# A graph-attention block with a quantised feed-forward on one core: the opening loads, the fill of the head pairs, the second layer norm and the last product rearranged

## The chip, the core and the metric

The kernel runs on one core of one Trainium2 chip. A core has five engines that run their own instruction streams and wait for one another by semaphores: TensorE (PE in the profile; its weight loads are PEld), VectorE (DVE), ScalarE (ACT), GpSimd (POOL) and SyncE (SP, which here only issues DMAs). The metric is the device time of one execution in microseconds (us). Three executions before the change took 384.24, 382.71 and 383.2 us; their median is 383.2 us.

## The reference

Inputs are x (384 x 1024), 6528 edges (`src`, `dst`, `edge_type_5`), and weights; all is f32.

```python
x = x + gnn(layernorm(x));  x = x + ffn(layernorm(x))

# gnn: q, k, v = x @ w.T + b, then a second projection each, 16 heads of 64
q2 = (q @ wiq.T + biq); k2 = (k @ wik.T + bik); v2 = (v @ wiv.T + biv)
mask = full((384, 384), -inf);  mask[src, dst] = softplus(edge_type_weights)[edge_type - 1]
# an empty diagonal place gets softplus(edge_type_weights)[3]; of equal edges the last one counts
attn = softmax(q2 @ k2.T / 8 + mask);  out = (attn @ v2) @ wo.T + bo

# ffn: fake quantisation of the activations by ONE scale over the whole tensor, weights row by row
def act_quant(x, clip): s = sigmoid(clip) * max(abs(x)) / 127; return clip(round(x / s), -128, 127) * s
h  = act_quant(silu(xq @ wg.T) * (xq @ wu.T), clip_down)       # xq = act_quant(x, clip_x), 352 wide
out = h @ wd.T
```

The scale over the whole tensor is a barrier: no element can be quantised before the largest of all is known.

## The kernel before

Rows are handled in three tiles of 128 (`NT`), features in eight blocks of 128 (`KC`). It runs in these stages.

**Opening (0 to 24 us).** SP issues the loads of x tile 0, x tile 1, `wq` blocks 0 and 1, x tile 2, and the other `wq` blocks (L83 to L87 and `load_w`), each 128 x 1024 f32 (512 KB). POOL issues seven small loads (L100 to L105): the rows of the biases, four edge-type weights and two clip factors, each of these three spread to all partitions by the DMA, and three lists of edges. While x arrives PE does 36 transposes of an identity (`WARM`). For each tile `row_stats` (L277) takes mean and reciprocal deviation on DVE (bn_stats, bn_aggr, `rstd_of`, whose square root is on ACT), and `normalise` (L284) writes the normalised rows on DVE (L288), turns them on PE four blocks at a time (L295) and copies each four from PSUM on ACT (L296). `q_first` (L300) multiplies the turned tile with `wq` blocks 0 and 1. The argument `between` puts the statistics of the next tile between the two groups of four; for tile 1 it is `edges_and_stats` (L317): edges to float, the key `384 * src + dst`, its way over memory back to all partitions (POOL, L323 and L257), and the statistics of tile 2.

**Projections (24 to 163 us).** `project2` (L178) computes two output blocks with seven products of half size in place of eight (Winograd's form of Strassen); `left_sums` and `right_sums` are its sums on DVE. Meanwhile DVE and POOL build the mask in memory (`tables`, `mask_groups`).

**Head pairs (163 to 333 us).** Eight pairs `p` of heads. PE's order is written out by hand: scores of pair p (L603) with softmax on DVE (L609, L623) and ACT (L613); transposes and weighted sums of pair p-1 (`weigh`, L633, L635, L641, L645); and between them `fill`, cut in sixteenths by `fill_to` (L694): for even p the product for v2 (L580), for odd p up to 5 the seven products of `inner_k` for the k2 of the next two pairs (L189, 29 steps), for p = 7 part of the output projection (L651). `prepare` puts the quantisation of the feed-forward weights in between (L496 to L542). The order on DVE and ACT in this stage follows from the program's order by a planner. The first product of `project2` goes from PSUM to SBUF on ACT (L203), and its PSUM buffer, one of two named mm, is the one that the third product writes.

**Output projection and second layer norm (333 to 357 us).** Per tile, PE finishes the output projection group by group (L801), and `residual` (L745) on DVE adds x and takes the row maximum (L747), bn_stats in pieces of 256 columns (L752) and the row minimum (L753); `normalise` (L755) ends with two DVE instructions per tile that write the normalised row (L787). Tile 2 has groups of 512, 256 and 256 columns in two PSUM buffers (mm). `turn` transposes each tile, `keep_busy` (L844) issues transposes whose result nobody reads, and `all_max` (L127) takes the largest value over all partitions.

**Feed-forward (357 to 384 us).** Gate and up products (L882), the second scale, and the product with wd (L929): six groups of 128 x 512, each scaled on DVE (L933), added to x on POOL (L938, first three) or DVE (L943, last three) into a tile `o` with three buffers, and stored by SP.

Of the kernel before, what the change touches and what calls it, by code (L numbers as in the profile page):

```python
# [23 lines left out]
F32 = mybir.dt.float32  # L24
# [37 lines left out]
def gnn_ffn_kernel(ctx: ExitStack, tc: tile.TileContext, a: dict, out: bass.AP):  # L62
# [18 lines left out]


    x = act.tile([P, NT, F], F32, name="actT")  # L83
    for t in range(NT):
        if t == NT - 1:
            wq_first = [load_w("wq", o) for o in range(FIRST)]
        nc.sync.dma_start(x[:, t, :], a["x"][t * P : (t + 1) * P, :])  # L87
    bias_rows = const.tile([5 * KC, P], F32)
    etw = const.tile([P, 4], F32)
    clip = const.tile([P, 2], F32)  # L90
    biv_b = const.tile([P, F], F32)


# [46 lines left out]

    ident_b = const.tile([P, P], BF16)
    later = ph1.tile([P, GROUP * P], F32, name="later", bufs=1)
    bias = const.tile([P, 5 * KC], F32)
    w8 = const.tile([P, 4], F32)

    def right_sums(src, pool, name, in_place=True):
# [90 lines left out]
    def run(steps):  # L237
        for _ in steps:
            pass
# [6 lines left out]
    with ph1_stack:  # L246
# [37 lines left out]
        def normalise(t, between=None):  # L284
            xn = rows_p.tile([P, F], F32, name="row")
            for j in range(2):
                hs = slice(j * 512, (j + 1) * 512)
                nc.vector.tensor_scalar(  # L288
                    xn[:, hs], x[:, t, hs], mv1[:, t, 0:1], rstd1[:, t : t + 1], op0=ALU.subtract, op1=ALU.mult
                )  # L290
            for g in range(2):
                pt = ps_tp.tile([P, 4, P], F32, name="tp")
                for j in range(4):
                    c = 4 * g + j
                    nc.tensor.transpose(pt[:, j, :], xn[:, c * P : (c + 1) * P], ident)  # L295
                nc.scalar.copy(xnT[:, 4 * g : 4 * g + 4, t * P : (t + 1) * P], pt)  # L296
                if g == 0 and between:
                    between()

# [10 lines left out]
        for _ in range(WARM):  # L310
            nc.tensor.transpose(pt, ident, ident)
        row_stats(0)
        normalise(0, lambda: row_stats(1))
        q_first(0, 0)
        q_first(1, 0)

        def edges_and_stats():  # L317

            nc.vector.tensor_copy(edges_f, edges_i)
# [8 lines left out]
        normalise(1, edges_and_stats)  # L328
        q_first(0, 1)
        q_first(1, 1)  # L330
        normalise(2)

        wneg = small.tile([P, 4], F32, name="wneg")
        nc.vector.tensor_scalar(wneg, etw, -1.0, None, op0=ALU.mult)
# [6 lines left out]
        pt = ps_tp.tile([P, 512], F32, name="tp")  # L341
        nc.tensor.transpose(pt[:, : 5 * KC], bias_rows, ident[: 5 * KC, : 5 * KC])
        wq_next = [load_w("wq", o) for o in (2, 3)]
        sums_next, steps = left_sums(*wq_next, ph1)
        run(steps)
        nc.vector.tensor_copy(bias, pt[:, : 5 * KC])
        x_right, steps = right_sums(xnT, ph1, "x_right", in_place=False)
        run(steps)
        q_first(0, 2)
# [194 lines left out]
    with ExitStack() as ph:  # L544
# [122 lines left out]
        for p in range(NP):  # L667
# [77 lines left out]
        def residual(t, col, c0, width, pm, st, hi, lo):  # L745
            cs = slice(c0, c0 + width)
            nc.vector.tensor_tensor_reduce(  # L747
                x[:, t, cs], pm[:, :width], x[:, t, cs], 1.0, -3.0e38, op0=ALU.add, op1=ALU.max,
                accum_out=hi[:, col : col + 1],
            )  # L750
            for c in range(c0, c0 + width, 256):
                nc.vector.bn_stats(st[:, c // 256, :], x[:, t, c : c + 256])  # L752
            nc.vector.tensor_reduce(lo[:, col : col + 1], x[:, t, cs], axis=AX.X, op=ALU.min)  # L753

        def normalise(t, last, st, hi, lo):  # L755

            mv = small.tile([P, 2], F32, name="mv2")
            nc.vector.bn_aggr(mv, st.rearrange("p a b -> p (a b)"))
            mean = mv[:, 0:1]
            var = small.tile([P, 1], F32, name="var2")  # L760
            nc.vector.tensor_scalar(var, mv[:, 1:2], EPS, None, op0=ALU.add)
            s0 = small.tile([P, 1], F32, name="s2")
# [12 lines left out]
            nw = small.tile([P, 1], F32, name="nw2")  # L775
            nc.vector.tensor_scalar(nw, vr, -0.5, 1.5, op0=ALU.mult, op1=ALU.add)
            rstd = small.tile([P, 1], F32, name="rstd2")
            nc.vector.tensor_mul(rstd, nw, r0)
            if t == 0:
                nc.vector.tensor_mul(row_max[:, 0:1], far, rstd)  # L780
            else:
                nc.vector.tensor_scalar(
                    row_max[:, t : t + 1], far, rstd, row_max[:, t - 1 : t], op0=ALU.mult, op1=ALU.max
                )
            for g in range(2):
                gs = slice(g * 512, (g + 1) * 512)
                nc.vector.tensor_scalar(xn[:, t, gs], x[:, t, gs], mean, rstd, op0=ALU.subtract, op1=ALU.mult)  # L787


        for t in range(NT):  # L790
            groups = [(0, 512), (512, 512)] if t < NT - 1 else [(0, 512), (512, 256), (768, 256)]
            st = small.tile([P, 4, 6], F32, name="st2")
            hi = small.tile([P, 3], F32, name="hi")
            lo = small.tile([P, 3], F32, name="lo")
            for g, (c0, width) in enumerate(groups):
                pm = open_groups.get((t, g)) if t < NT - 1 else None
                ks = [NP - 1]
                if pm is None:
                    pm, ks = ps_mm.tile([P, 512], F32, name="mm"), range(KC)
                for k in ks:  # L800
                    nc.tensor.matmul(  # L801
                        pm[:, :width], outT[:, k, t * P : (t + 1) * P], wo[k][:, c0 : c0 + width],
                        start=(k == 0), stop=(k == KC - 1),
                    )
                residual(t, g, c0, width, pm, st, hi, lo)
                if g == 1 and len(groups) == 3:
                    nc.vector.tensor_tensor(hi[:, 0:1], hi[:, 0:1], hi[:, 1:2], op=ALU.max)
                    nc.vector.tensor_tensor(lo[:, 0:1], lo[:, 0:1], lo[:, 1:2], op=ALU.min)
            normalise(t, len(groups) - 1, st, hi, lo)
        run(prep)  # L810

# [1 line left out]
    with ExitStack() as ph:  # L813
# [109 lines left out]
        for t in range(NT):  # L923
            ts = slice(t * P, (t + 1) * P)
            for g in range(2):
                gs = slice(g * 512, (g + 1) * 512)
                pm = ps_mm.tile([P, 512], F32, name="mm")
                for ic, (i0, rows) in enumerate(ICS):
                    nc.tensor.matmul(  # L929
                        pm, hq[:rows, ic, ts], wdT[:rows, ic, gs], start=(ic == 0), stop=(ic == 2)  # L930
                    )
                y = ff.tile([P, 512], F32, name="y", bufs=6)
                nc.vector.scalar_tensor_tensor(y, pm, sh, wd_scale_b[:, gs], op0=ALU.mult, op1=ALU.mult)  # L933
                if len(last) or t * 2 + g == 3:
                    last.append((t, gs, y))
                else:
                    o = ff.tile([P, 512], F32, name="o")
                    nc.gpsimd.tensor_add(o, x[:, t, gs], y)  # L938
                    nc.sync.dma_start(out[t * P : (t + 1) * P, gs], o)

        for t, gs, y in last:
            o = ff.tile([P, 512], F32, name="o")
            nc.vector.tensor_add(o, x[:, t, gs], y)  # L943
            nc.sync.dma_start(out[t * P : (t + 1) * P, gs], o)


# [45 lines left out]
```

## Time and profile before

| what | value |
|---|---|
| median of three executions | 383.2 us (382.71 to 384.24) |
| the profiled execution | 385.56 us, of which the span is 383.8 us |
| PE busy, share of the span | 364.5 us, 95% |
| DVE, ACT, POOL busy | 261.1, 107.2, 74.6 us |
| granted TensorE clock, mean | 0.986 of full speed |
| read from memory | 41.91 MB |

Times in the profile count from the start of the span. "Busy" of PE is modelled from pipelined matmuls, so that a wait inside a group shows as a longer group. A line like `[3.67 <-ACT k L203]` gives the time that an engine stood idle before an instruction and what released it. The chain of waits is followed back from the last instruction; 70% of it is PE, 14% DVE, 7% DMA and 5% ACT.

### The profile page before, as it was taken

Reading aid. Unit: us, or ns where it says so; the run is one execution under the profiler, and the core shown is the slowest. Engines: PE = TensorE matmul, PEld = TensorE weight load, DVE = VectorE, ACT = ScalarE, POOL = GpSimd, SP = SyncE. Lnnn points to the kernel's source line nnn. Section 1 sums busy time; section 2 is a strip of 40 time slices with the busy share of each in tenths; the row PEclk is TensorE's granted clock in tenths of the full one; section 3 lists DMA queues with packets and bytes.
Section 4 is the critical chain, followed back from the end, with each engine's and each line's share of the span. In section 5 each row is a group of like instructions: output and inputs, shape, how many; then the busy total and the mean of one; then the engine's idle time right before and its main releaser. Section 6 shows DMA issues by size and latency. Waiting matters only on the chain.

```text
span 383.8 us, 5838 instructions
## 1 busy us (share of the span) xinstructions
PE 364.5 (95%) x2101; PEld 301.2 (78%) x2101; DVE 261.1 (68%) x785; ACT 107.2 (28%) x256; POOL 74.6 (19%) x81
## 2 busy tenths in 40 slices
PE   7999999999999999989879999999999999998973
PEld 7899999999999998987676859686776545457661
DVE  5878888888879987976657366726583430298784
ACT  2252100000000010144553545536443524001330
POOL 6100354455545543400000000000000000000003
PEclk9999999999999999999989999999999999999996
DMA  8996333343343456283440030140394000000004
GB/s 239 375 397 212 114 111 110 113 130 111 110 123 110 145 174 206 57 273 106 146 129 3 19 130 19 38 147 0 118 371 130 6 0 2 0 0 1 2 1 164
DMA packets 17804, 44.50 MB, mean 116 GB/s; under 512 B 3262, under 2 KB 8400, under 8 KB 17392
## 3 DMA queue, kind: packets, MB, share of 16 engines
q1 hardware_dynamic: 15104, 39.46, 30.5%
q0 software_dynamic: 2672, 4.68, 4.1%
q8 instruction: 16, 0.26, 0.3%
q14 instruction: 12, 0.10, 0.1%
HBM read 41.91 MB, written 2.21 MB: 115 GB/s over the span
## 4 chain that ended last, share of the span: by engine, by line
PE 70%; DVE 14%; DMA 7%; ACT 5%; issue 2%; POOL 0%; SPq 0%; DVEq 0%; ACTq 0%
PE p L189 33%; PE mm L580 7%; PE mm L189 6%; PE tp L633 4%; PE mm L651 3%; PE sc L651 3%; PE mm L303 3%; PE sc L641 3%; PE sc L603 3%; DMA row<-in_L_ffn_w_down_dram 2%; DMA wt<-in_wik_dram 2%; ACT e L613 2%; DVE e L623 2%; DVE s L609 1%; DMA row<-in_L_ffn_w_gate_dram 1%
## 5 line engine op out<-in xcount | busy, mean ns | idle before, releaser
L425 POOL DMA_INDIRECT mask_d<-value,place x51 | 59.3, 1162 | 62.1 <-DVE place L422 47.0
L189 PE MATMUL p<-actT,wt 128*128 128x192 f32 x360 | 65.8, 326 | 0.0
L189 PEld LDWEIGHTS p<-actT,wt 128*128 128x128 f32 x360 | 59.7, 190 | 0.0
L580 PE MATMUL mm<-wt,actT 128*128 128x256 f32 x192 | 46.1, 384 | 0.0
L580 PEld LDWEIGHTS mm<-wt,actT 128*128 128x128 f32 x192 | 34.8, 190 | 7.8 <-issue 2.2
L613 ACT ACTIVATE e<-s,mn 128x384 f32<-128x384 f32 x48 | 29.0, 605 | 31.1 <-DVE mn L609 29.5
L609 DVE CUSTOM_DVE_ANT_0 s<-sc,mask 128x384 f32<-128x384 f32 x48 | 24.6, 550 | 13.1 <-PE sc L603 13.0
L818 POOL MEMSET hT<- 128x384 f32 x1 | 0.4, 418 | 163.7 <-PE sc L641 163.7
L189 PE MATMUL p<-x_right,s 128*128 128x192 f32 x176 | 32.2, 326 | 0.0
L189 PE MATMUL p<-x_right,wt 128*128 128x192 f32 x176 | 32.2, 326 | 0.0
L189 PEld LDWEIGHTS p<-x_right,s 128*128 128x128 f32 x176 | 29.2, 190 | 0.0
L189 PEld LDWEIGHTS p<-x_right,wt 128*128 128x128 f32 x176 | 29.2, 190 | 0.0
L635 ACT COPY eTs<-tp 128x384 f32<-128x384 f32 x48 | 20.7, 481 | 28.0 <-PE tp L633 27.9
L412 DVE SCALAR_TENSOR_TENSOR junk<-key_b,key,later 128x384 f32<-128x384 f32 (+3 forms) x51 | 27.5, 540 | 0.0
L200 DVE SCALAR_TENSOR_TENSOR actT<-p,bias,actT 128x192 f32<-128x192 f32 x45 | 18.7, 416 | 8.5 <-PE p L189 4.8
L189 PE MATMUL mm<-actT,wt 128*128 128x192 f32 x96 | 20.7, 344 | 4.0 <-ACT k L203 4.0
L203 ACT COPY actT<-p 128x192 f32<-128x192 f32 x15 | 4.8, 320 | 66.1 <-PE p L189 66.1
L189 PEld LDWEIGHTS mm<-actT,wt 128*128 128x128 f32 x96 | 15.9, 196 | 8.3 <-ACT k L203 4.9
L603 PE MATMUL sc<-k,actT 64*128 64x384 f32 x96 | 21.7, 521 | 0.1
L633 PEld LDWEIGHTS tp<-ident,e 128*128 128x128 f32 x144 | 17.2, 141 | 5.0 <-issue 2.6
L213 ACT ACTIVATE actT<-p,bias 128x192 f32<-128x192 f32 x15 | 6.3, 421 | 52.7 <-PE p L189 34.8
L633 PE MATMUL tp<-ident,e 128*128 128x128 f32 x144 | 20.0, 275 | 0.3 <-ACT eTs L635 0.3
(210 smaller groups left out, 589.7 us busy)
## 6 DMA issues: line engine op xcount, KB each, us to landing
wt<-in_wq_dram SPq DMA_DIRECT2D x8, 512.0 KB
wt<-in_wk_dram SPq DMA_DIRECT2D x8, 512.0 KB
wt<-in_wv_dram SPq DMA_DIRECT2D x8, 512.0 KB
wt<-in_wiq_dram SPq DMA_DIRECT2D x8, 512.0 KB
wt<-in_wik_dram SPq DMA_DIRECT2D x8, 512.0 KB
wt<-in_wiv_dram SPq DMA_DIRECT2D x8, 512.0 KB
wt<-in_wo_dram SPq DMA_DIRECT2D x8, 512.0 KB
actT<-in_x_dram SPq DMA_DIRECT2D x6, 512.0 KB
```

The costliest lines, as they stand in the source:

```text
L189: nc.tensor.matmul(z, left[:, k * P : (k + 1) * P], r[:, k, :], start=(k == 0), stop=(k == HK - 1))
L200: nc.vector.scalar_tensor_tensor(dst, z, b, with_, op0=ALU.add, op1=ALU.add)
L303: nc.tensor.matmul(pm_first[o][:, ts], wq_first[o][:, k * P : (k + 1) * P], xnT[:, k, ts], start=(k == 0), stop=(k == KC - 1),)
L412: nc.vector.scalar_tensor_tensor(junk[:, :left], keys[:, (c - k0) * P : (c - k0) * P + left], key[:, c : c + 1], later[:, :left], op0=ALU. ...
L425: ins = nc.gpsimd.indirect_dma_start(out=mask_d, out_offset=bass.IndirectOffsetOnAxis(ap=place[:, c : c + 1], axis=0), in_=value[:, c : c ...
L580: nc.tensor.matmul(pm, vT[:, k, t * P : (t + 1) * P], wt[k // HK][:, k0 : k0 + 256], start=(k == 0), stop=(k == KC - 1),)
L603: nc.tensor.matmul(ps[t, h], q2[hs, t * P : (t + 1) * P], k2[hs, :], start=True, stop=True)
L609: nc.vector.tensor_tensor_reduce(s, ps[t, h], mask[:, t, :], -SCALE, 3.0e38, op0=ALU.add, op1=ALU.min, accum_out=mn[h][:, t : t + 1],)
L613: nc.scalar.activation(e[h][:, t, :], s, AF.Exp, bias=mn[h][:, t : t + 1], scale=-1.0, accum_out=sm[h][:, t : t + 1],)
L633: nc.tensor.transpose(pt[:, t * P : (t + 1) * P], e[h][:, t, m * P : (m + 1) * P], ident)
L635: nc.scalar.copy(eT[h][m], pt)
L651: nc.tensor.matmul(pm, outT[:, k, t * P : (t + 1) * P], wo[k][:, gs], start=(k == 0), stop=(k == KC - 1))
```

## The change

- *Opening.* x tile 0 is loaded as two halves of 64 partitions, the lower by SP and the upper by ACT. POOL's seven small loads move behind the statistics of tile 1: a POOL copy of tile 1's mean and variance (`loaded`) comes first, then the edges, the biases, the weights and the clip factors. The last two go into one row of six numbers on one partition, and a matmul with a row of ones spreads them over the partitions, into the PSUM tile that holds the turned biases; one DVE copy takes both. Tile 0's copies from PSUM (L296) are cut in two. The edge work moves behind the statistics of tile 2.
- *Head pairs.* `fill_to(2)` becomes `fill_to(3)` for odd p.
- *Second layer norm.* bn_stats takes 512 columns at once for tiles 0 and 1. Their normalised rows are written by ACT in two passes (subtract, then scale), after one small DVE instruction for the negated mean. Tile 2 is cut into 512, 256, 128 and 128 columns, the last two in other PSUM buffers (sc), with bn_stats of 128 columns. The first `keep_busy` has 14 transposes and not 18.
- *Last product.* The groups alternate between PSUM buffers mm and x, and the sums are written over `y`, without the tile `o`.

```diff
+    half = P // 2
+    nc.scalar.dma_start(x[half:, 0, :], a["x"][half:P, :])
     for t in range(NT):
         if t == NT - 1:
             wq_first = [load_w("wq", o) for o in range(FIRST)]
-        nc.sync.dma_start(x[:, t, :], a["x"][t * P : (t + 1) * P, :])
+        rows = half if t == 0 else P
+        nc.sync.dma_start(x[:rows, t, :], a["x"][t * P : t * P + rows, :])
...
-    nc.gpsimd.dma_start(bias_rows, a["biases"])
-    nc.gpsimd.dma_start(etw, row_bcast(a["L0_gnn_edge_type_weights"], 4))
-    nc.gpsimd.dma_start(clip[:, 0:1], row_bcast(a["L0_ffn_clip_x"], 1))
-    nc.gpsimd.dma_start(clip[:, 1:2], row_bcast(a["L0_ffn_clip_down"], 1))
-    for j, name in enumerate(("src", "dst", "edge_type_5")):
-        nc.gpsimd.dma_start(edges_i[:, j, :], a[name].rearrange("(c p) -> c p", p=P))
+    nc.gpsimd.memset(ones, 1.0)
...
-                nc.scalar.copy(xnT[:, 4 * g : 4 * g + 4, t * P : (t + 1) * P], pt)
+                step = 2 if t == 0 else 4
+                for j in range(0, 4, step):
+                    c = 4 * g + j
+                    nc.scalar.copy(xnT[:, c : c + step, t * P : (t + 1) * P], pt[:, j : j + step, :])
...
-        normalise(0, lambda: row_stats(1))
+        def stats_and_loads():
+            row_stats(1)
+            loads = [(edges_i[:, j, :], a[n].rearrange("(c p) -> c p", p=P)) for j, n in enumerate(("src", "dst", "edge_type_5"))]
+            loads.append((bias_rows, a["biases"]))
+            for c0, n, name in ((0, 4, "L0_gnn_edge_type_weights"), (4, 1, "L0_ffn_clip_x"), (5, 1, "L0_ffn_clip_down")):
+                loads.append((row[:, c0 : c0 + n], a[name].rearrange("(a n) -> a n", a=1)))
+            nc.gpsimd.tensor_copy(loaded, mv1[:, 1, :])
+            for dst, src in loads:
+                nc.gpsimd.dma_start(dst, src)
+        normalise(0, stats_and_loads)
...
-        def edges_and_stats():
+        def stats_and_edges():
+            row_stats(2)
             nc.vector.tensor_copy(edges_f, edges_i)
...
-            row_stats(2)
...
         normalise(2)
+        pt = ps_tp.tile([P, 512], F32, name="tp")
+        nc.tensor.transpose(pt[:, :NB], bias_rows, ident[:NB, :NB])
+        nc.tensor.matmul(pt[:, NB : NB + 6], ones, row, start=True, stop=True)
...
+        nc.vector.tensor_copy(bias, pt[:, : NB + 6])
...
-            fill_to(2)
+            fill_to(3 if p % 2 else 2)
             prepare(2)
             next(sc)
...
-            for c in range(c0, c0 + width, 256):
-                nc.vector.bn_stats(st[:, c // 256, :], x[:, t, c : c + 256])
+            for c in range(c0, c0 + width, part):
+                nc.vector.bn_stats(st[:, c // part, :], x[:, t, c : c + part])
...
+            if t < NT - 1:
+                minus = small.tile([P, 1], F32, name="minus")
+                nc.vector.tensor_scalar(minus, mean, -1.0, None, op0=ALU.mult)
             for g in range(2):
                 gs = slice(g * 512, (g + 1) * 512)
-                nc.vector.tensor_scalar(xn[:, t, gs], x[:, t, gs], mean, rstd, op0=ALU.subtract, op1=ALU.mult)
+                if t < NT - 1:
+                    nc.scalar.activation(xn[:, t, gs], x[:, t, gs], AF.Identity, bias=minus)
+                    nc.scalar.activation(xn[:, t, gs], xn[:, t, gs], AF.Copy, scale=rstd)
+                else:
+                    nc.vector.tensor_scalar(xn[:, t, gs], x[:, t, gs], mean, rstd, op0=ALU.subtract, op1=ALU.mult)
...
-            groups = [(0, 512), (512, 512)] if t < NT - 1 else [(0, 512), (512, 256), (768, 256)]
+            if t < NT - 1:
+                groups, part = [(0, 512), (512, 512)], 512
+            else:
+                groups, part = [(0, 512), (512, 256), (768, 128), (896, 128)], 128
...
-                    pm, ks = ps_mm.tile([P, 512], F32, name="mm"), range(KC)
+                    pool, name = (ps_mm, "mm") if g < 2 else (ps_sc, "sc")
+                    pm, ks = pool.tile([P, 512], F32, name=name), range(KC)
...
-        keep_busy(18, ps_x, "x")
+        keep_busy(14, ps_x, "x")
...
-                pm = ps_mm.tile([P, 512], F32, name="mm")
+                pool, name = (ps_mm, "mm") if g == 0 else (ps_x, "x")
+                pm = pool.tile([P, 512], F32, name=name)
...
-                    o = ff.tile([P, 512], F32, name="o")
-                    nc.gpsimd.tensor_add(o, x[:, t, gs], y)
-                    nc.sync.dma_start(out[t * P : (t + 1) * P, gs], o)
+                    nc.gpsimd.tensor_add(y, x[:, t, gs], y)
+                    nc.sync.dma_start(out[t * P : (t + 1) * P, gs], y)
...
-            o = ff.tile([P, 512], F32, name="o")
-            nc.vector.tensor_add(o, x[:, t, gs], y)
-            nc.sync.dma_start(out[t * P : (t + 1) * P, gs], o)
+            nc.vector.tensor_add(y, x[:, t, gs], y)
+            nc.sync.dma_start(out[t * P : (t + 1) * P, gs], y)
```

In the planner's order after the change, ACT's copy L203 of an odd pair stands behind the first two exponentials of that place and ahead of the other four; before, six (p = 1) or five (p = 3, 5) exponentials stand ahead of it.

More of the change, by code (lines that the diff above doesn't have):

```diff
@@ L86, in gnn_ffn_kernel @@
             wq_first = [load_w("wq", o) for o in range(FIRST)]
-        nc.sync.dma_start(x[:, t, :], a["x"][t * P : (t + 1) * P, :])
+        rows = half if t == 0 else P
+        nc.sync.dma_start(x[:rows, t, :], a["x"][t * P : t * P + rows, :])
     bias_rows = const.tile([5 * KC, P], F32)
-    etw = const.tile([P, 4], F32)
-    clip = const.tile([P, 2], F32)
+    row = const.tile([1, 6], F32)
+    ones = const.tile([1, P], F32)
     biv_b = const.tile([P, F], F32)
@@ L142, in gnn_ffn_kernel @@
     later = ph1.tile([P, GROUP * P], F32, name="later", bufs=1)
-    bias = const.tile([P, 5 * KC], F32)
+    NB = 5 * KC
+    bias = const.tile([P, NB + 6], F32)
+    etw, clip = bias[:, NB : NB + 4], bias[:, NB + 4 : NB + 6]
     w8 = const.tile([P, 4], F32)
@@ L312, in gnn_ffn_kernel @@
         row_stats(0)
-        normalise(0, lambda: row_stats(1))
+        def stats_and_loads():
[7 more added lines that the diff above has]
+                nc.gpsimd.dma_start(dst, src)
+        loaded = small.tile([P, 2], F32, name="loaded")
+        normalise(0, stats_and_loads)
         q_first(0, 0)
         q_first(1, 0)
-        def edges_and_stats():
+        def stats_and_edges():
+            row_stats(2)
             nc.vector.tensor_copy(edges_f, edges_i)
@@ L325, in edges_and_stats @@
                 load_keys()
-            row_stats(2)
-        normalise(1, edges_and_stats)
+        normalise(1, stats_and_edges)
         q_first(0, 1)
@@ L331, in gnn_ffn_kernel @@
         normalise(2)
+        pt = ps_tp.tile([P, 512], F32, name="tp")
+        nc.tensor.transpose(pt[:, :NB], bias_rows, ident[:NB, :NB])
+        nc.tensor.matmul(pt[:, NB : NB + 6], ones, row, start=True, stop=True)
+        wq_next = [load_w("wq", o) for o in (2, 3)]
+        sums_next, steps = left_sums(*wq_next, ph1)
+        run(steps)
+        nc.vector.tensor_copy(bias, pt[:, : NB + 6])
         wneg = small.tile([P, 4], F32, name="wneg")
@@ L340, in gnn_ffn_kernel @@
         nc.scalar.activation(wln, wexp, AF.Ln, bias=1.0)
[L341 to L346, printed above, removed]
         x_right, steps = right_sums(xnT, ph1, "x_right", in_place=False)
@@ L743, in gnn_ffn_kernel, with residual @@
         open_groups = {(t, g): pm for t, g, pm in early}
-        def residual(t, col, c0, width, pm, st, hi, lo):
+        def residual(t, col, c0, width, part, pm, st, hi, lo):
             cs = slice(c0, c0 + width)
@@ L784, in normalise @@
                 )
+            if t < NT - 1:
+                minus = small.tile([P, 1], F32, name="minus")
+                nc.vector.tensor_scalar(minus, mean, -1.0, None, op0=ALU.mult)
             for g in range(2):
                 gs = slice(g * 512, (g + 1) * 512)
-                nc.vector.tensor_scalar(xn[:, t, gs], x[:, t, gs], mean, rstd, op0=ALU.subtract, op1=ALU.mult)
-        for t in range(NT):
-            groups = [(0, 512), (512, 512)] if t < NT - 1 else [(0, 512), (512, 256), (768, 256)]
-            st = small.tile([P, 4, 6], F32, name="st2")
-            hi = small.tile([P, 3], F32, name="hi")
-            lo = small.tile([P, 3], F32, name="lo")
+                if t < NT - 1:
[3 more added lines that the diff above has]
+                    nc.vector.tensor_scalar(xn[:, t, gs], x[:, t, gs], mean, rstd, op0=ALU.subtract, op1=ALU.mult)
+        for t in range(NT):
+            if t < NT - 1:
+                groups, part = [(0, 512), (512, 512)], 512
+            else:
+                groups, part = [(0, 512), (512, 256), (768, 128), (896, 128)], 128
+            st = small.tile([P, F // part, 6], F32, name=f"st2_{part}")
+            hi = small.tile([P, 4], F32, name="hi")
+            lo = small.tile([P, 4], F32, name="lo")
             for g, (c0, width) in enumerate(groups):
@@ L804, in gnn_ffn_kernel @@
                     )
[L805 to L808, printed above, removed]
+                residual(t, g, c0, width, part, pm, st, hi, lo)
+                if 0 < g < len(groups) - 1:
+                    nc.vector.tensor_tensor(hi[:, 0:1], hi[:, 0:1], hi[:, g : g + 1], op=ALU.max)
+                    nc.vector.tensor_tensor(lo[:, 0:1], lo[:, 0:1], lo[:, g : g + 1], op=ALU.min)
             normalise(t, len(groups) - 1, st, hi, lo)
@@ L933, in gnn_ffn_kernel @@
                 nc.vector.scalar_tensor_tensor(y, pm, sh, wd_scale_b[:, gs], op0=ALU.mult, op1=ALU.mult)
-                if len(last) or t * 2 + g == 3:
+                if t * 2 + g >= 3:
                     last.append((t, gs, y))
                 else:
-                    o = ff.tile([P, 512], F32, name="o")
-                    nc.gpsimd.tensor_add(o, x[:, t, gs], y)
-                    nc.sync.dma_start(out[t * P : (t + 1) * P, gs], o)
+                    nc.gpsimd.tensor_add(y, x[:, t, gs], y)
+                    nc.sync.dma_start(out[t * P : (t + 1) * P, gs], y)
         for t, gs, y in last:
-            o = ff.tile([P, 512], F32, name="o")
-            nc.vector.tensor_add(o, x[:, t, gs], y)
-            nc.sync.dma_start(out[t * P : (t + 1) * P, gs], o)
+            nc.vector.tensor_add(y, x[:, t, gs], y)
+            nc.sync.dma_start(out[t * P : (t + 1) * P, gs], y)
 def _out_blocks(w):
```

## The prediction

> **What bounds the kernel now.** I read the page first, for the shares; then the waits and the chain of waits, for the places where TensorE (PE) stands still; then the timeline and the windows around these places.
>
> ```profile
> span 383.8 us, 5838 instructions
> PE 364.5 (95%) x2101; PEld 301.2 (78%) x2101; DVE 261.1 (68%) x785; ACT 107.2 (28%) x256; POOL 74.6 (19%) x81
> PE 70%; DVE 14%; DMA 7%; ACT 5%; issue 2%; POOL 0%; SPq 0%; DVEq 0%; ACTq 0%
> ```
>
> PE is busy for 95% of the span: an edit is worth the PE idleness, or half-speed PE time, that it removes. Four stretches show that and are touched: the opening, the first product of the odd head pairs, the second layer norm with the scale behind it, and the last product. The timeline at pair 1 (start, us, engine, line, operation, and in brackets the idle time before it with its releaser):
>
> ```profile
> 189.46 1.46 PE L189 MATMUL mm<-k_right,s 128*128 128x192 f32 x8
> 194.59 0.92 PE L189 MATMUL mm<-actT,wt 128*128 128x192 f32 x4 [3.67 <-ACT k L203]
> 197.46 2.33 PE L189 MATMUL mm<-actT,s 128*128 128x192 f32 x8
> 199.62 0.60 PE L633 MATMUL tp<-ident,e 128*128 128x128 f32 x4
> 193.64 0.60 ACT L613 ACTIVATE e<-s,mn 128x384 f32<-128x384 f32 x1
> 194.24 0.29 ACT L203 COPY k<-mm 128x192 f32<-128x192 f32 x1
> ```
>
> PE idles 3.67 us until ACT's copy L203 frees a PSUM buffer; that copy, 0.29 us long, is queued behind exponentials whose scores come late from DVE. The windows beside it (PE, PEld, DVE, ACT, POOL busy; granted clock; DMA share; GB/s):
>
> ```profile
> 191.00:194.60 3.60, 0.01 (x1) 0.01 (x1) 2.99 (x11) 2.84 (x10) 0.00 (x0) 1.00 0.11 44
> 195.80:199.20 3.40, 3.40 (x14) 3.40 (x13) 1.44 (x3) 0.96 (x2) 0.00 (x0) 0.50 0.69 217
> 374.00:375.00 1.00, 1.00 (x4) 0.30 (x2) 0.13 (x2) 0.00 (x0) 1.00 (x2) 0.50 0.00 0
> ```
>
> The stall is followed by 3.4 us of PE work at a granted clock of 0.50; the last product runs at 0.50 too. Then, on PE and DVE, the stalls of later pairs, the second layer norm and the last product, and links of the chain of waits:
>
> ```profile
> 227.48 2.59 PE L603 MATMUL sc<-k,actT 64*128 64x384 f32 x8
> 262.62 1.94 PE L603 MATMUL sc<-k,actT 64*128 64x384 f32 x8
> 348.21 3.72 PE L801 MATMUL mm<-wt,actT 128*128 128x256 f32 x16 [1.61 <-DVE hi L747]
> 373.44 4.37 PE L929 MATMUL mm<-wdT,hq 128*128 128x512 bf16 x12 [0.19 <-DVE y L933]
> 378.52 1.88 DVE L943 TENSOR_TENSOR o<-actT,y 128x512 f32<-128x512 f32 x3
> ...
> 353.68 1.97 PE x L848 x18
> 355.75 1.11 PE mm L842 x8
> ```
>
> Opening: the first tile's load heads the chain, and POOL's queue holds the small loads. From the chain, the windows and the timeline:
>
> ```profile
> 0.73 3.37 DMA actT<-in_x_dram
> 3.00:4.00 1.00, 1.00 (x7) 1.00 (x6) 0.00 (x0) 0.00 (x0) 1.00 (x3) 1.00 0.99 373
> 11.98 0.35 DVE L319 CAST edges_f<-edges_i 51x384 f32<-51x384 int32 x1 [0.19 <-DMA edges_i<-in_edge_type_dram]
> 18.25 1.63 POOL L257 DMA_DIRECT2D key_b<-key_row_d  x3 [4.76 <-DMA key_row_d<-key_row]
> 19.40 0.25 PE L342 MATMUL tp<-ident,bias_rows 40*128 40x40 f32 x1 [0.24 <-ACT actT L296]
> ```
>
> **The sum is made against the profiled execution, 385.56 us (span 383.8), and then moved to the median of the runs, 383.2, which is 2.4 lower.**
>
> **1. Opening: 0.** Tile 0 lands at 4.10. The windows move 53 GB/s in 1 to 2 us, 307 in 2 to 3, 373 in 3 to 4 and 393 in 4 to 5. That is 512 KB by about 3.44, and 1 MB by about 4.8. If the halves get the engines first, the gain is 0.6; if both halves interleave with tile 1, the loss is 0.7. The transfer before ends in the middle, so 0. The Trainium skill, DMA: Bandwidth & Descriptors, Rules for kernel authors, says that two transfers to disjoint partition halves are not worth making, since they share the same 16 engines. The window at 373 GB/s with a DMA share of 0.99 agrees, and by that rule the gain would be 0.
>
> The halved copy L296 stands on the chain: 512 columns take 0.57 and 192 columns (L203) 0.32, so 256 about 0.37, and PE starts 0.2 earlier after it (−0.2). The new matmul with a row of ones is one more on PE; its neighbour L342 took 0.25, the lower bound is a 0.10 transpose: +0.15. The new copy of one more row of columns in L346 stays at about 0.20.
>
> The small loads are the risk. POOL's `loaded` copy waits for tile 1's statistics, about 9.3; then seven issues at 0.54 each (L103, L105): src 9.4, dst 9.95, type 10.5, then biases, weights, clip factors to about 13. Nearest rows for issue to use: the key row, issued 12.95, gives way to L257 at 18.25 (5.2); the type load, issued 4.95 in a crowd, was used at 11.98 (7.0). So type is there at 15.2 to 17.5. DVE needs it at 16.9, because L319 (0.35), L320 (0.28) and the first half row (0.54) then follow, and PE's transposes of tile 2 stand at 18.12. The clip factors land at 17.7 to 19.9; PE needs them at 19.4. I take 5.2 (the queue is emptier at 10 us than at 5) and no wait; the other end is +0.6 and +0.5. Behind a late L319, DVE would hold the row of tile 2 (L288), and PE the transposes. The key row and its three spreads shift by 2 to 3 us, hidden: their first reader on DVE, L412, starts at 36.39. The scalars wneg and wnab (0.16 each) now come behind the bias copy, ahead of x_right, which PE wants at 25.07: hidden; without that cover +0.3. On SP, the loads of wq behind x are one entry later and find PE busy to 24. ACT's added issue stands beside its table load (first root needed at 5.87). Opening: 0, bounds −0.8 to +1.9.
>
> **2. First product of pair 1 (`fill_to(3)`): −3.8.** Three more or two more steps go ahead of the next scores, so L203 stands behind two exponentials and ahead of the others. Before: the next transposes L633 at 199.62. After: product 1, all eight matmuls now ahead of the scores, ends near 187.65 (186.02 and eight at 0.2, the 1.24 of six); L203 waits for one exponential (188.05 to 188.65) and perhaps the copy L534 (0.77 in the row at 188.65), so 188.95 at the latest; product 2 (1.46) ends near 191.1; the first transposes need e, which DVE normalises by 192.1 (L623 x3 at 190.85 ends 191.92, and the int8 cast L504, 0.69, now stands ahead); product 4 needs L206, behind four score steps L609 of 0.55, at about 194.3, and ends at 195.8. So 3.8. Of it 3.67 is the idle and about 1.7 is the second half of the half-speed stretch (3.41 at 0.50), less 1.6 that PE then waits for DVE. Lower end: the wait for DVE eats all but the shorter queue, 1.5. Upper end: DVE keeps up, 4.5. Next late: DVE, through L206. L496, which waits for a w_down row on DMA (0.80 at 188.68), stands ahead of L206 and can hold it.
>
> **3. Pairs 3, 5, 7: −1.7.** Eight score matmuls take 1.56 undisturbed (at 187.54) and 2.59, 1.94 and 2.16 (at 227.48, 262.62, 297.73): 1.04, 0.38, 0.60 more, and 0.19 in a wait for L203 at 232.08. They wait for DVE's copy L645 behind L623. With the filled steps placed ahead, I take 0.7, 0.5 and 0.5. Bounds 0 (DVE is simply late) and 2.4.
>
> **4. Second layer norm and scale: −1.8.** DVE is the chain from 333.74 to 348.2. Two bn_stats of 256 (0.75) become one of 512 (half of L280's 1.28, 0.64): four times 0.11 to 0.15. L787 x2 (0.92) leaves DVE for tiles 0 and 1, for one `minus` (0.15) each: 0.6 + 1.84 − 0.3 = 2.1. The residual L747 of tile 2 starts at 345.4 instead of 347.55. PE's 1.61 wait at 348.21 was for the PSUM buffer that this reads; the last two groups now have other buffers. So its last 16 matmuls, of 256 columns before (3.72), can start at 346.6 (348.21 less 1.61), as 32 of 128 columns; L303's run at 0.12 (32 in 3.84 in the chain), so 3.9, and they end near 350.5 instead of 351.93. The last residual block is 128 wide: 0.75 of L747, L752 and L753 for 1.13 at 256; the aggregate reads more sets (+0.1). So row_max comes 1.7 earlier. PE's turns (0.87 x2) and 14 in place of 18 idle transposes (1.53 for 1.97) then reach L129 at 353.8 for 355.64. ACT's two passes (four of 0.57 per tile) run under DVE's 6.9 us a tile; the last transposes of tile 1 come at 351.77. Bounds: 1.0 (PE or ACT late with the turned rows), 2.3 (all of DVE's saving and the wait).
>
> **5. Last product: −0.5.** PE at 0.50 took 4.37 for twelve matmuls. A PSUM wait of 0.19 goes, and with a second buffer DVE's y no longer holds PE: y5 (377.85) and L943 come 0.45 earlier, if the clock stays at 0.50. The in-place sum removes no step. Bounds 0 and −1.9 (PE not the bound: six y at 0.70 from 372.64 give 376.7 for 378.5).
>
> **Sum:** 0 − 3.8 − 1.7 − 1.8 − 0.5 = −7.8, so 377.8 profiled and **375.4** as median.
>
> **The half-clock stretches.** They last 3.41 us (195.8 to 199.2 and 373.29 to 376.70). The Trainium skill, TensorE: Matmul & The Clock Gate, What's actually happening, describes a free-running window of 3413 ns and a slow window after an idle one. The trace agrees, 3.41 after an idle 3.67, and 1.81 idle before 371.78. By it the last product may fall in a fast window, an effect of phase that gives rival (b).
>
> **The rivals.**
> (a) *The stall only changes its releaser.* DVE, 2.99 of 3.60 busy in the window of the idle, is nearly full, so e and L206 come late whatever ACT does, and PE waits as long for them. For it: L206 stands behind four L609 and L504. Against: product 2 and transposes fit in between. Steps 2 and 3 give 1.5 and 0.5: 375.4 + 2.3 + 1.2 = 378.9.
> (b) *The last product misses the half-clock stretch.* Six y at 0.70 are step 5's upper bound, −1.9 for −0.5: 374.0. For it: the phase shifts by 7 us. Against: the idle before it (1.8) stays.
> (c) *The opening loses.* Halves interleave (+0.7), type lands 7.0 after issue (+0.6): 376.7.
> (d) *Slower than before: late small loads.* PE's tile-2 transposes wait for DVE's L319; each us beyond 16.9 is one of time. It must eat 7.8 + 1.9 = 9.7, so type lands at 26.6, 16 us after issue, against 5.2 and 7.0 in rows: not spoken for.
> (e) *The filled steps do nothing.* ACT's first two exponentials at that place themselves come late from DVE, and L203 with them; steps 2 and 3 give nothing, and step 4 its lower bound, since the same DVE sets it: 381.7. Against: these two ended at 188.65.
>
> **How the numbers follow.** 0.5% is 1.9 us, about what a measurement of this kernel can tell from no change: 381.3 and 385.1 are the bounds. Chances: forecast 0.43, (a) 0.23, (b) 0.13, (c) 0.10, (d) 0.04, (e) 0.07. Case (e) is "same", 0.07; (d) is slower, 0.04; the rest is faster, 0.89. The range holds the forecast, (a), (b) and (c): from 374.0 less 1.0 for the upper ends of steps 2 and 3, to 378.9 plus 0.8 for the lower end of step 4 and 0.8 for an opening late by (c)'s kind: 373.0 to 380.5.
>
> **What would show it.** Right: no idle above 1 us before L189 near 190 to 195 and no 0.50 window behind it; L633 at least 3 us earlier there; score groups of pairs 3 to 7 under 1.9; the wait at L801 gone, L129 1.8 earlier relative to the 333.7 start; y six in a row. Wrong: a wait by PE for DVE (e or L206) of 2 us or more at pair 1; a DMA as releaser of L319 behind 17; ACT as releaser of L842.

## The result and the profile after

The changed kernel takes 376.73 us (median of six, 376.37 to 377.56) against 383.16 us for the kernel before it on the same chip (382.20 to 384.79): the ratio is 0.983, with an interval of 0.9805 to 0.9854. The forecast was 375.4, with a range of 373.0 to 380.5.

The profiled execution of after took 376.78 us (span 375.0), which is the median. That of before took 385.56 (span 383.8), 2.4 above its median, so the two profiles differ by 8.8 us where the medians differ by 6.4. The experiments below bear on where the 2.4 lie. First the page of after, then the longest waits of PE between 155 and 325 us (engine, operation and what it waited for: us in total, times, longest):

```profile
span 375.0 us, 5879 instructions
PE 359.8 (96%) x2115; PEld 300.3 (80%) x2115; DVE 260.3 (69%) x788; ACT 112.9 (30%) x266; POOL 72.1 (19%) x83
PE 77%; DVE 12%; DMA 6%; ACT 3%; issue 1%; DVEq 0%; SPq 0%; ACTq 0%
...
PE mm L190 <- DVE k L207: 0.8, 1, 0.8
PE p L190 <- DVE s L172: 0.8, 1, 0.8
PE tp L652 <- ACT eTs L654: 0.3, 1, 0.3
```

PE's share of the chain went from 70% to 77% and ACT's from 5% to 3%; the wait of 3.7 us for ACT's copy (L203, now L204) is gone from the list. The timeline at pair 1, some lines of PE and then of ACT:

```profile
188.39 0.49 PE L190 MATMUL mm<-k_right,s 128*128 128x192 f32 x2
190.64 1.24 PE L190 MATMUL mm<-k_right,s 128*128 128x192 f32 x6
191.72 0.81 PE L190 MATMUL mm<-actT,wt 128*128 128x192 f32 x4
194.65 1.57 PE L190 MATMUL mm<-actT,s 128*128 128x192 f32 x8 [0.81 <-DVE k L207]
196.06 0.82 PE L652 MATMUL tp<-ident,e 128*128 128x128 f32 x6
...
188.34 0.60 ACT L632 ACTIVATE e<-s,mn 128x384 f32<-128x384 f32 x1
188.94 0.29 ACT L204 COPY k<-mm 128x192 f32<-128x192 f32 x1
192.93 0.62 ACT L632 ACTIVATE e<-s,mn 128x384 f32<-128x384 f32 x1 [0.26 <-DVE mn L628]
```

ACT's copy now runs at 188.94, behind two exponentials, and not at 194.24 behind all of them. PE idles once, 0.81 us for DVE's L207, the wait that the prediction named as next. The turns of e that began at 199.62 begin at 196.06. The first score group of the kernel begins 0.97 later than in the profile of before (173.42 there), so pair 1 gave 4.5. Next the clock (windows: us, then PE, PEld, DVE, ACT, POOL busy, clock, DMA share, GB/s) and the score groups of pairs 3, 5 and 7:

```profile
196.00:200.00 4.00, 4.00 (x31) 3.96 (x30) 3.40 (x8) 2.21 (x6) 0.00 (x0) 1.00 0.43 144
...
224.56 1.56 PE L622 MATMUL sc<-k,actT 64*128 64x384 f32 x8
258.38 1.56 PE L622 MATMUL sc<-k,actT 64*128 64x384 f32 x8
292.87 1.56 PE L622 MATMUL sc<-k,actT 64*128 64x384 f32 x8
```

The clock is 1.00 where before it was 0.50, and each score group takes the undisturbed 1.56. The chain of waits through the second layer norm, and through the opening:

```profile
326.52 1.72 PE mm L833 x4
329.95 10.32 PE mm L833 x32
340.27 3.58 PE sc L833 x32
346.57 0.27 DVE row_max L802
347.36 1.13 PE mm L874 x8
348.51 0.75 DVE x L903
...
0.72 4.99 DMA actT<-in_x_dram
5.81 1.30 DVE st L281 x2
25.72 118.32 PE p L190 x728
```

The layer norm is now PE's, without a gap from 326.52 to 343.85; from its first matmul in the chain (332.84 before, 326.52 after) to DVE's first rounding (356.89 and 348.51) it takes 21.99 for 24.05. Other traces repeat both: 24.04 with the old layer norm (the split alone, below) and 21.99 with the new one (everything but the filled steps); which of its edits gives how much, no run separates. The opening is worse: tile 0 lands at 5.71 for 4.10, and the first p starts at 25.72 for 23.93. Last, the end of the program: the last sums of GpSimd and DVE, and the instructions of the program's closing line (duration min/median/max in ns, first and last start):

```profile
365.10 3.71 POOL L970 TENSOR_TENSOR y<-actT,y 128x512 f32<-128x512 f32 x3 [16.47 <-DVE y L966]
368.22 2.35 DVE L974 TENSOR_TENSOR y<-actT,y 128x512 f32<-128x512 f32 x3
...
L1019 POOLq DRAIN  x3: 46/103/7843, 366.4 to 374.7; - x3
L1019 SPq DRAIN  x3: 7/7/7, 373.2 to 374.5; - x3
```

GpSimd's queue sits in a drain of 7.84 us that ends at 374.2; SP, which waits for the outputs, is done at 373.2. In the profile of before SP was the later of the two: 383.0, with GpSimd's drain ending at 382.6. So the ledger of the two profiles is: up to the first scores +0.97, pair 1 −4.54, pairs 3, 5, 7 −1.32, −0.82 and −0.61, layer norm and scale −2.06, last product to the end −0.42 (11.16 to 10.74 from the first y): −8.8.

### The profile page after: what moved, and what is told of

Read it like the earlier page. It is cut to its first block, busy times and chain, and to the rows that moved or that the text cites. A ratio compares the mean times of both kernels' runs of the same rounds, so it can differ in the third digit from the quotient of the medians.

```text
span 375.0 us, 5879 instructions
## 1 busy us (share of the span) xinstructions
PE 359.8 (96%) x2115; PEld 300.3 (80%) x2115; DVE 260.3 (69%) x788; ACT 112.9 (30%) x266; POOL 72.1 (19%) x83
## 4 chain that ended last, share of the span: by engine, by line
PE 77%; DVE 12%; DMA 6%; ACT 3%; issue 1%; DVEq 0%; SPq 0%; ACTq 0%
PE p L190 34%; PE mm L599 7%; PE mm L190 7%; PE tp L652 4%; PE sc L660 4%; PE sc L622 4%; PE mm L670 3%; PE sc L670 3%; PE mm L833 3%; PE mm L308 3%; DMA row<-in_L_ffn_w_gate_dram 2%; DVE wmx L515 2%; DMA row<-in_L_ffn_w_up_dram 1%; PE sc L833 1%; DMA actT<-in_x_dram 1%; DVE s L628 1%
## 5 line engine op out<-in xcount | busy, mean ns | idle before, releaser
L444 POOL DMA_INDIRECT mask_d<-value,place x51 | 56.6, 1110 | 64.8 <-DVE place L441 53.2
L204 ACT COPY actT<-p 128x192 f32<-128x192 f32 x15 | 4.8, 318 | 66.1 <-PE p L190 66.1
L622 PE MATMUL sc<-k,actT 64*128 64x384 f32 x96 | 19.9, 518 | 0.0
L190 PE MATMUL mm<-actT,wt 128*128 128x192 f32 x96 | 18.9, 329 | 0.0
L642 DVE TENSOR_SCALAR e<-e,rs 128x384 f32<-128x384 f32 x48 | 17.2, 415 | 0.4
```

The costliest lines, as they stand in the source:

```text
L190: nc.tensor.matmul(z, left[:, k * P : (k + 1) * P], r[:, k, :], start=(k == 0), stop=(k == HK - 1))
L444: ins = nc.gpsimd.indirect_dma_start(out=mask_d, out_offset=bass.IndirectOffsetOnAxis(ap=place[:, c : c + 1], axis=0), in_=value[:, c : c ...
L622: nc.tensor.matmul(ps[t, h], q2[hs, t * P : (t + 1) * P], k2[hs, :], start=True, stop=True)
L642: nc.vector.tensor_scalar(e[h][:, t, :], e[h][:, t, :], rs[:, t : t + 1], None, op0=ALU.mult)
```

## The experiments

Each time is a median of six executions or more. The kernels ran in four sets, each on one chip; sets are compared through the kernel before, whose medians in them were 384.06 (first four runs), 384.17 (next four), 384.27 (next three) and 384.44 (last).

**The filled steps alone.**

```diff
-            fill_to(2)
+            fill_to(3 if p % 2 else 2)
```

> The kernel before, with only fill_to(3) for odd pairs. By the two profiles the pairs gained 4.54 (pair 1), 1.32, 0.82 and 0.61, 7.3 in all. Theory A (1.7 of these are the half-speed stretch behind pair 1's wait, which not every execution has): time 383.2 less 5.6, 377.6, and transposes of pair 1 about 4.5 earlier than in the profile before. Theory F (the whole 7.3 belongs to the edit): 375.9. The prediction's sizes (3.8 and 1.7) gave 377.7.

Measured 378.08, ratio 0.984 (0.981 to 0.988): 6.0 less than before beside it. In its profile the last turns of e come 7.4 earlier than in the profile of before. The gain itself is clear: the six executions lie between 377.77 and 378.61, while those of before lie between 382.26 and 387.07. The two theories are not told apart: 6.0 is nearer to A's 5.6 than to F's 7.3, but the interval of the ratio reaches from 4.6 to 7.4 us. The edit does two things, it puts more of PE's steps ahead of the scores and with them ACT's copy ahead of the exponentials; no run moves the copy alone. In pair 7, which has no such copy, the steps alone go with the 0.61 of the ledger.

**Everything but the filled steps.**

```diff
-            fill_to(3 if p % 2 else 2)
+            fill_to(2)
```

> The changed kernel with fill_to(2) for every pair, as before. If the filled steps carry the gain: 376.9 plus 5.5 to 6.3, 382.4 to 383.2, PE's wait of 3 us or more for ACT's copy L204 back at pair 1, in some executions with a half-speed stretch behind it, and executions spread over 3 us or more where the changed kernel's spread is 1 to 2.6. If opening, layer norm and last product carried it: below 380.

Measured 383.00 (381.96 to 385.46 in twelve), 0.9975 of before (0.9951 to 0.9998): nearly all of the gain is gone. Its profiled execution, 382.06, was one of its quickest. PE's timeline and the window behind the wait:

```profile
195.50 0.92 PE L190 MATMUL mm<-actT,wt 128*128 128x192 f32 x4 [3.37 <-ACT k L204]
...
196.00:200.00 4.00, 4.00 (x30) 3.96 (x29) 2.33 (x6) 2.30 (x6) 0.00 (x0) 1.00 0.59 178
```

The wait of 3.37 is back, but the clock behind it is 1.00, where the profile of before had 3.67 and then 3.4 us at 0.50. So one execution had the wait without the half-speed stretch. The trace of the kernel before with the split alone (below) has both, in PE's timeline and its window:

```profile
196.44 1.65 PE L192 MATMUL mm<-actT,wt 128*128 128x192 f32 x4 [3.23 <-ACT k L206]
...
196.00:200.00 4.00, 3.56 (x13) 3.47 (x14) 0.52 (x2) 2.40 (x6) 0.00 (x0) 0.50 0.35 102
```

That the stretch costs 1.7 more where it falls in is read from the profiles of before and of this run. How often it falls in is not shown for each execution, but the mean granted clocks speak for it. Of 55 executions of the kernel before, the 13 with 0.982 to 0.987 have a median of 385.66 us and the 11 with 0.994 or 0.995 one of 382.26. The 66 executions of the versions with the filled steps have 0.991 to 0.998, and their times do not follow the clock. The executions of this run spread over 3.5 us, but those of versions with the filled steps over 0.8 to 3.4, so the stretch is not all that spreads them. Pair 1 is 1.97 us shorter in this trace than in that of before, and 4.54 shorter in that of after: without a slow stretch on either side, the filled steps give 2.6 there. The Trainium skill, TensorE: Matmul & The Clock Gate, What's actually happening, says that the windows run free of the kernel; a wait about as long as one window that is at times followed by a slow one and at times not agrees with that.

**Tile 0 whole, and the split alone.** The first is the changed kernel without the split; the second is the kernel before with it.

```diff
-    half = P // 2
-    nc.scalar.dma_start(x[half:, 0, :], a["x"][half:P, :])
...
-        rows = half if t == 0 else P
-        nc.sync.dma_start(x[:rows, t, :], a["x"][t * P : t * P + rows, :])
+        nc.sync.dma_start(x[:, t, :], a["x"][t * P : (t + 1) * P, :])
```

> The changed kernel, with tile 0 of x loaded whole on SP's queue. Theory A (the split delays tile 0 by 1.6 us, and about 0.8 of that is absorbed at the loads that DVE waits for between 142 and 174 us): tile 0 lands near 4.1 instead of 5.7, the first p of L190 starts near 24.1 instead of 25.7, the score group of the first pair comes about 1.0 earlier, time 375.7. Rival B (the late opening is the small loads', DVE's wait of 0.91 for the edge types): tile 0 lands at 4.1, but the first p starts at 25 or later. Rival C (any delay of the opening is absorbed later): the first p earlier, time 376.7 within 0.3.

> The kernel before, with only the split of tile 0 on two queues. Theory A: tile 0 lands near 5.7 instead of 4.1, PE's first p of L189 starts 1.2 to 1.6 later than 23.93, time about 1.0 longer, 384.2. Rival C (absorbed): tile 0 late, time 383.2. Rival D (the delay came of the emptied POOL queue or of this execution, not of the split): tile 0 lands at 4.1, no change.

Without the split: 375.93, ratio to before 0.978 (0.9745 to 0.982), 0.8 under the changed kernel by the medians, 1.7 by what each gains on the kernel before beside it; the intervals of the two ratios overlap. The split alone: 385.86, ratio 1.0041 (1.001 to 1.0073), slower. Both signs are theory A's. In windows and chain, first of the whole tile in the changed kernel, then of the changed kernel itself:

```profile
4.00:5.00 1.00, 1.00 (x6) 1.00 (x5) 0.89 (x2) 0.00 (x0) 0.00 (x0) 1.00 0.98 381
...
24.04 3.09 PE p L187 x19
```

```profile
4.00:5.00 1.00, 1.00 (x6) 1.00 (x5) 0.00 (x0) 0.00 (x0) 0.00 (x0) 1.00 1.15 193
```

The engines are as busy (1.15 for 0.98) and move half as much in this execution. They do not in each. The run with two sums on GpSimd (below) has the same opening; its window, and DVE's start on tile 0:

```profile
4.00:5.00 1.00, 1.00 (x10) 1.00 (x9) 0.00 (x0) 0.00 (x0) 0.00 (x0) 1.00 1.02 324
...
5.15 1.29 DVE L281 BATCH_NORM_STATS2 st<-actT 128x6 f32<-128x512 f32 x2 [4.29 <-DMA actT<-in_x_dram]
```

Over all traces the statistics of tile 0 start at 5.11 to 5.81 with the partition halves (seven traces) and at 4.02 to 4.21 with the tile whole (six). With the halves nothing is moved before 2 us, with the whole tile 29 to 86 GB/s between 1 and 2 us; between 4 and 5 us it is 148 to 344 GB/s against 340 to 393. So the late tile is shown in each trace, and the lower rate explains only a part of it.

In the kernel before the split costs 1.8 by the medians, more than the 1.0 expected. Why is not shown: PE waits 2.35 us there for tile 0's rows (0.91 in the changed kernel), and the profiled execution had a slow stretch right behind that wait. Its first product and the window beside it are

```profile
10.52 5.53 PE mm L306 x32
...
11.00:14.00 3.00, 3.00 (x16) 2.95 (x15) 2.52 (x11) 0.68 (x2) 0.00 (x0) 0.50 1.04 414
```

that is 5.53 for 32 matmuls that take 3.84 at full clock.

**Both halves on one queue; halves by columns.**

```diff
-    nc.scalar.dma_start(x[half:, 0, :], a["x"][half:P, :])
+    nc.sync.dma_start(x[half:, 0, :], a["x"][half:P, :])
```

> The changed kernel with both halves of tile 0 on SP's queue (upper half first), none on ACT's. Theory Q (what costs is a second queue: the halves and the tiles behind them share the engines packet by packet): DVE's first bn_stats starts near 4.4, as without the split, against 5.4 to 6.1 with it, and the time is that of the run without the split, 0.8 below the changed kernel. Theory H (transfers of 64 rows are slow in themselves): first bn_stats at 5.3 or later, time 376.7 to 377.0.

```diff
-        nc.sync.dma_start(x[:, t, :], a["x"][t * P : (t + 1) * P, :])
+        for c in ((0, F // 2) if t == 0 else (0,)):
+            cs = slice(c, c + F // 2) if t == 0 else slice(0, F)
+            nc.sync.dma_start(x[:, t, cs], a["x"][t * P : (t + 1) * P, cs])
```

> The changed kernel with tile 0 in two halves of 512 columns, 128 partitions each, both on SP's queue. Theory H1 (what costs in the halves is that only 64 partitions are written at a time): in the window of 4 to 5 us the engines move 350 GB/s or more, as with the whole tile (381), where the partition halves moved 148 and 193; tile 0's statistics start at 4.1 to 4.4 or earlier, time 375.9 within 0.4. Theory H2 (any second transfer for the tile costs): the windows of 3 to 5 us stay under 320 GB/s, statistics at 5 or later, time 376.7 or more.

Measured 377.76 (ratio 0.984, 0.981 to 0.988) and 375.83 (0.979, 0.974 to 0.984). Windows and DVE's timeline, first for one queue, then for the columns:

```profile
4.00:5.00 1.00, 1.00 (x6) 1.00 (x5) 0.00 (x0) 0.00 (x0) 0.00 (x0) 1.00 0.90 148
...
5.51 1.29 DVE L281 BATCH_NORM_STATS2 st<-actT 128x6 f32<-128x512 f32 x2 [4.66 <-DMA actT<-in_x_dram]
```

```profile
3.00:4.00 1.00, 1.00 (x7) 1.00 (x6) 0.58 (x1) 0.00 (x0) 0.14 (x1) 1.00 0.84 193
4.00:5.00 1.00, 1.00 (x8) 1.00 (x7) 0.46 (x2) 0.00 (x0) 0.00 (x0) 1.00 1.03 244
...
3.42 0.69 DVE L280 BATCH_NORM_STATS2 st<-actT 128x6 f32<-128x512 f32 x1 [2.57 <-DMA actT<-in_x_dram]
4.66 0.69 DVE L280 BATCH_NORM_STATS2 st<-actT 128x6 f32<-128x512 f32 x1 [0.54 <-DMA actT<-in_x_dram]
```

One queue is no better than two (5.51, within the 5.11 to 5.81 of the halves), so theory Q falls: the second queue is not the cause. The columns also move slowly (193 and 244 GB/s), which theory H1 didn't expect, and the tile is whole 0.5 later than when loaded at once; but its first half is there at 3.42, half of the statistics run early, and the time is that of the whole tile, against H2. So two transfers for the tile are slower than one in both ways of cutting it, and the partition halves are the worse, since DVE's statistics take all 128 partitions and can start on neither. What delays the tile stays open.

**The opening of before, and the small loads first.** The first run is the changed kernel with the whole opening of before; the second has tile 0 whole and only the loads moved back.

```diff
+    nc.gpsimd.dma_start(bias_rows, a["biases"])
+    for c0, n, name in ((0, 4, "L0_gnn_edge_type_weights"), (4, 1, "L0_ffn_clip_x"), (5, 1, "L0_ffn_clip_down")):
+        nc.gpsimd.dma_start(row[:, c0 : c0 + n], a[name].rearrange("(a n) -> a n", a=1))
+    for j, name in enumerate(("src", "dst", "edge_type_5")):
+        nc.gpsimd.dma_start(edges_i[:, j, :], a[name].rearrange("(c p) -> c p", p=P))
     nc.gpsimd.memset(ones, 1.0)
...
-            nc.gpsimd.tensor_copy(loaded, mv1[:, 1, :])
-            for dst, src in loads:
-                nc.gpsimd.dma_start(dst, src)
```

> The changed kernel with the opening of before, whole. Theory A: first p at 23.9, time about 1.0 below the changed kernel, 375.7. Rival B (the small loads behind tile 1's statistics are what costs, not the split): this one is lower than the run without the split by 0.5 or more. Rival C (absorbed): 376.7. If the rest of the opening (halved copies, spread by a product) gains, this one is higher than the run without the split.

> The changed kernel with tile 0 whole on SP's queue and GpSimd's seven small loads first, as before; edge work still behind the statistics of tile 2. Theory O (what the rest of the opening gains is the order: statistics of tile 2 no longer wait for the edge types on DVE): same as the run without the split, 375.9 within 0.4, first p at 24.0 to 24.5. Theory M (the moved loads gain by leaving the engines to x): x lands later, first p at 24.6 or later as with the opening of before, 376.5.

Measured 376.64 and 376.14. By the medians the whole new opening is thus worth nothing (376.73 with it, 376.64 without), and without the split 0.5 to 0.7, which is of the size of the executions' spread. What the new order changes is seen in DVE's timeline with the opening of before:

```profile
12.81 0.35 DVE L319 CAST edges_f<-edges_i 51x384 f32<-51x384 int32 x1 [1.05 <-DMA edges_i<-in_edge_type_dram]
13.20 0.28 DVE L320 SCALAR_TENSOR_TENSOR key_row<-edges_f 51x128 f32<-51x128 f32 x1
13.41 0.68 DVE L280 BATCH_NORM_STATS2 st<-actT 128x6 f32<-128x512 f32 x1
```

The statistics of tile 2 wait there for the edge types, 1.05 us. In the changed kernel DVE waits 0.91 for the same loads, but at 17.77, with tile 2's statistics done and PE at work until 19.60; with the loads first and tile 0 whole it doesn't wait for them at all. But PE's first p does not come earlier for it: in the chains it starts at 24.04, 24.11 and 24.30 in the three traces with the new order and tile 0 whole, and at 23.93, 24.16 and 24.53 in the three with the opening of before. So a gain of the order is not shown, though theory O's numbers came true (376.14, and the first p at 24.11 where theory M needed 24.6). Moving the loads neither gains nor costs measurably.

**The end.** The changed kernel again, with the last product of before, and with one more of the six last sums on DVE and one less on GpSimd:

```diff
-                if t * 2 + g >= 3:
+                if t * 2 + g >= 2:
                     last.append((t, gs, y))
```

> The changed kernel again, unchanged, as the measure for the three beside it on one chip: 376.7 within 0.4. Every theory: first p near 25.7; last add of GpSimd, then 5.4 us of its drain, then the end.

> The changed kernel with the last product of before (two PSUM buffers, tile o, no sum in place). Theory P (at full clock the end is set by GpSimd: its third add ends, its drain ends 5.4 us later, and the program 0.7 after that; the DVE side has slack): from the first y to the end 10.7 us as in the changed kernel, time the same within 0.3. The prediction's step 5 (the last y and the three sums of DVE set the end): 0.5 to 1.1 longer, since y takes 4.7 and not 4.0 and the sums 2.7 and not 2.3.

> The changed kernel with two of the six last sums on GpSimd and four on DVE, where it had three and three. Theory P: GpSimd's chain ends 1.2 earlier, and the end is then set by SP's last output, which has 1.1 of slack now: time 0.9 to 1.1 less than the changed kernel beside it. Rival (the last output sets the end): DVE has one more sum of 0.6, less 0.46 of its slow first one: 0.1 to 0.3 longer.

Measured 377.06, 377.07 and 376.43. The last product's change is worth nothing, as theory P has it: from the first y to the end it is 10.7 either way. It brings the end of SP 0.8 nearer to the first y (8.9 for 9.7), but GpSimd's drain ends 10.0 behind it in both. In the profile of before, whose last product ran at half clock, the whole stretch took 11.16. With two sums on GpSimd, its timeline, DVE's, and the closing line:

```profile
365.17 2.50 POOL L970 TENSOR_TENSOR y<-actT,y 128x512 f32<-128x512 f32 x2 [16.46 <-DVE y L966]
368.29 2.49 DVE L974 TENSOR_TENSOR y<-actT,y 128x512 f32<-128x512 f32 x4
...
L1019 POOLq DRAIN  x3: 46/103/7283, 365.8 to 373.9; - x3
L1019 SPq DRAIN  x3: 7/7/7, 373.3 to 373.6; - x3
```

GpSimd's drain ends 5.4 us behind its last sum (367.67 to 373.1; in the changed kernel 368.81 to 374.2), so it moves with the sum, and SP's output is last again. From the first y to the end: 9.87 for 10.74. The median moved by 0.63 for the 0.9 to 1.1 expected, within the spread, so that the gain rests on the trace.

**Both repairs:** tile 0 whole, and two sums on GpSimd.

> Both repairs: tile 0 whole on one queue, and two sums on GpSimd. If they add up: 0.8 and 1.0 below the changed kernel beside it, near 374.9. If the drain theory is wrong, like the run without the split, 375.9.

Measured 374.53 (374.06 to 376.81), ratio 0.977 (0.972 to 0.982): 2.5 under the changed kernel beside it, where 1.8 was expected, and 1.9 under two sums alone on the same chip, which is one more measure of the split. It is the quickest version here.

## Why the prediction was right, and where it was not

The sign and the size were right (−7.8 forecast, −6.4 measured), and most of it is where it was put: in the copy L203 and what stood ahead of it on ACT. That the totals lie so near is partly luck. Between the two profiles steps 2 to 5 gave 9.8 for the 7.8 forecast and the opening took back 1.0; 2.4 of the remaining 8.8 are what the profiled execution of before had over its median.

- *Step 1, opening, 0.* Within its bounds in sum (0.97 later at the first scores), but not by its mechanism. The step that failed is "the transfer before ends in the middle, so 0". Its bounds, a gain of 0.6 and a loss of 0.7, assumed that the engines keep their 373 to 393 GB/s. Tile 0 came 1.6 later in the profile and 0.9 to 1.8 over the traces: with the split the first bytes moved later, and the rate fell, to 193 GB/s in this profile and to 324 or 344 in the mildest traces. Of the 1.8 at the first p about half was gone by the first scores (0.97), in a stretch that waits for weights. That the order of tile 2's statistics gave anything back is not shown. The rule of the Trainium skill that such halves aren't worth making (DMA: Bandwidth & Descriptors, Rules for kernel authors) gave 0 too; it speaks against the split, and the runs go further than it does: here the halves cost 0.8 us or more. The late loads were no danger: the edge types, issued at 12.66, were used at 17.77, 5.1 later (5.2 taken), and PE didn't wait. The halved copies brought PE 0.2 nearer to tile 0's turns, as put.
- *Step 2, −3.8.* The mechanism was right, with copy, order and next wait. Between the profiles it is 4.5, the upper bound, since the wait for L207 was 0.81 where 1.6 had been put. For the median the term was mis-sized by its base: 1.7 of it was a half-speed stretch that the profiled execution of before had and that of everything but the filled steps had not; without the stretch it is 2.6.
- *Step 3, −1.7.* 2.75, over its upper bound of 2.4: I took 0.7 of pair 3's 1.04 + 0.19, and it gave all of it and 0.1 more; pairs 5 and 7 gave 0.82 and 0.61 for 0.5 each.
- *Step 4, −1.8.* 2.06, and PE without a gap at L833, as worked out.
- *Step 5, −0.5.* The profiles have −0.42, but that the number fits is luck. The step that failed is that DVE's y and sums set the end. In the profile of before, at half clock, they were last by only 0.4 (SP 383.0, GpSimd's drain 382.6). At equal clock the change gives nothing, since GpSimd's third sum and its drain end later than the outputs.
- *Rivals.* (a) fell: PE's wait for DVE was 0.81. (b) came true in the profile of after, where the last product ran at full clock, but gained 0.4 and not 1.9, for the reason of step 5. (c) was right in that tile 0 came late, whether by interleaving or not; the edge types came in time for PE. (d) and (e) didn't occur.

## What to carry to other kernels

An instruction of a few tenths of a microsecond that frees a buffer may stand behind a queue of work which waits for another engine: moving it a few places ahead, by way of the PE work that it follows, was worth some 6 us here with what this freed in the later pairs, more than all the other edits together. Work out a stall's price from several executions when a half-speed stretch can follow it, since one profile may hold such a stretch and another not. And ask which engine is last at the very end of the program, its closing drain included, before making another one faster.

## What was not expected of the hardware

- Tile 0 as one transfer of 512 KB could be used from 4.0 to 4.2 us (six traces), as two of 256 KB cut by partitions from 5.1 to 5.8 (seven), and its second half cut by columns from 4.7 (one). Between 4 and 5 us the DMA engines, equally busy (0.88 to 1.15), moved 340 to 393, 148 to 344 and 244 GB/s.
- GpSimd's closing drain ended 5.4 us behind its last sum in each trace looked at (before, after, the filled steps alone, two sums), so that a sum of 1.24 us on GpSimd can cost more at the end of a program than one of 0.6 on DVE.
- DVE's first sum took 1.06 us in the chain of the changed kernel, while GpSimd's third was running for the first 0.5 of it, and the others 0.60: three sums took 2.35, and four, with GpSimd done, 2.49.
